# Selective-scan macaron block: the state sums of two scan units issued as a pair

## The chip, the core and the metric

The kernel runs on one core of a Trainium2 chip. The metric is the device time of one execution in microseconds (us), the median of three runs. The core's engines work from queues of their own, each in order: TensorE (PE, with its weight loads PEld), VectorE (DVE), ScalarE (ACT), GpSimd (POOL) and SyncE (SP), which issues nearly all the transfers. They wait for one another by semaphores.

## What is computed

The input x has 4 sequences of 1024 tokens with 512 channels, in fp32. Three stages follow one another, each added to its input:

```python
x = x + 0.5 * ffn(layernorm(x))        # gate/up 512 -> 1408, silu(g) * u, down 1408 -> 512
x = x + attn(layernorm(x))             # the selective scan below
x = x + 0.5 * ffn(layernorm(x))        # the same weights again
# attn, for I = 1024 inner channels and N = 16 states:
h, gate = split(x @ W_in.T); h = silu(conv4(h) + conv_b)
ts, Bm, Cm = rms-normed parts (128, 16, 16) of h @ Wx.T
delta = softplus(ts @ Wdt.T + dt_bias)
s[t] = exp(delta[t] * A) * s[t-1] + delta[t] * Bm[t] * h[t]     # for each channel and state
y[t] = sum over the 16 states of s[t] * Cm[t]  + D * h[t]
out  = (y * silu(gate)) @ Wout.T
```

The line that matters here is the sum over the 16 states.

## The kernel before

The 4096 tokens are cut into 16 blocks of T = 256 (NCS = 16, four to a sequence). The inner channels are cut into NI = 8 tiles of 128. The scan lays four states of 32 channels on the 128 partitions (Q = 32, S = 4), so a tile i of a block k needs NS = 4 groups g of states; one `unit(k, i, g)` handles 4 states of all 128 channels, as four strips of 32 channels. A block has 32 units, the kernel 512.

A unit (L553 to L587) goes, in two halves: ACT makes exp(delta * A) into the PSUM tile `da` (L569), POOL makes delta * B * u into `sb` (L572), DVE scans along the tokens in place in `da` (`tensor_tensor_scan`, L576), ACT keeps the last column as `state` (L581), and DVE multiplies by C into the unit's tile `pr` (L584). `pr` has four buffers, `da` four halves. The unit is then put on the list `summed`.

`add_up` (L591 to L600) takes the oldest unit off that list. PE sums its states: four matmuls, one per strip j, of the 128 x 32 matrix `fold` against 256 columns of `pr`; each writes 32 partitions of the PSUM tile `yps`, in which the four g of a tile accumulate (L594). The two halves of `yps` alternate from tile to tile. Behind the fourth g, DVE adds D * u and brings the result to `u` (L600). `gated` (L604, POOL) multiplies by the silu of the gate.

Beside the scan of block k stands a background (`background`, L694): the products of the first FFN for later token tiles and of the second FFN for earlier ones (gate L269 with its eviction by ACT at L283, up L269 with DVE at L300, down L315 with DVE at L323), the gate part of W_in for the block (gp, L541, eviction L545), the output product of block k-1 (op, L623, L627), and the preparation of block k+1: transposes of the normed input (L231), the conv part of W_in (hp, L372) with its first tap on ACT (L376) and three more on DVE (L383), the product with Wx (sp, L407), its norm (ACT L425, POOL L428 to L430, DVE L436), transposes (L449, L450) whose results DVE copies (L451, L452), and `head`, the softplus with the product dp (L486). Products take PSUM from three buffers (`ps_m`).

The loop at L792 to L823 sets the order: it issues a unit, then perhaps a sum, then as many pieces of the background as keep pace with the work done, by costs in PE and DVE work. A recording layer then schedules the instructions of each engine from that order, so that single matmuls may change places with their neighbours. Before, `BEHIND = 2` (L33): a sum is issued behind the unit that is two further on.

```python
                if len(summed) > BEHIND:
                    add_up()
```

The list is not emptied between blocks, only at the end of the last one (L824).

Of the kernel before, what the change touches and what calls it, by code (L numbers as in the profile page):

```python
# [29 lines left out]
BC = 2 * N  # L30
RO = R + BC
HEAD = 10
BEHIND = 2  # L33
LEAD = 12
BEGUN = 7
RING = 14
# [3 lines left out]
def macaron_kernel(ctx: ExitStack, tc: tile.TileContext, a: dict, out: bass.AP):  # L40
# [119 lines left out]
    def settle():  # L160
        while deferred:
            deferred.pop(0)[1]()

    def do(w):
        if w.settled:
            settle()
        before = list(deferred) if w.cost else []
        if w.blocks:
            got = given.pop(id(w))
            assert len(got) == len(w.blocks)  # L170
            w.emit(got)
        else:
            w.emit()
        passed(before)
        held.pop(id(w), None)
        fetch()
        for x in stores:
            x[0] += 1
        write(2)
# [293 lines left out]
    def head(k, i):  # L473

        d = st[k]
        nm = f"{k}_{i}"
        dp = ps_m.tile([P, 2, T], F32, tag="mm", name=f"dp{nm}")
        z = p1.tile([P, 2, T], F32, tag="z", name=f"z{nm}")
        e = p1.tile([P, 2, T], F32, tag="e", name=f"e{nm}")
        lg = p1.tile([P, 2, T], F32, tag="lg", name=f"lg{nm}")  # L480
        dd = p2.tile([P, 2, 2, T], F32, tag="dd", name=f"dd{nm}")
        de = dd[:, :, 0, :]

        def products():
            for q in range(2):
                nc.tensor.matmul(  # L486
                    dp[:, q, :], lhsT=w_dt[:, (i + q) * P : (i + q + 1) * P], rhs=d["tsT"],
                    start=True, stop=True,
                )

        def split():
            for q in range(2):
                b = dt_b[:, i + q : i + q + 1]
                pin(nc.scalar.activation(z[:, q, :], dp[:, q, :], AF.Abs, bias=b))
                pin(nc.scalar.activation(dd[:, q, 0, :], dp[:, q, :], AF.Relu, bias=b))

        def logs():
            pin(nc.scalar.activation(z, z, AF.Exp, scale=-1.0))  # L498
            pin(nc.scalar.activation(lg, z, AF.Ln, bias=1.0))

        def correct():
            pin(nc.gpsimd.tensor_tensor(e, e, z, ALU.subtract))
            pin(nc.gpsimd.tensor_tensor(lg, lg, e, ALU.subtract))

        def complete():
            pin(nc.gpsimd.tensor_tensor(de, de, lg, ALU.add))
            pin(nc.gpsimd.tensor_tensor(dd[:, :, 1, :], de, d["u"][:, i : i + 2, :], ALU.mult))
            d["dd", i] = dd[:, 0]
            d["dd", i + 1] = dd[:, 1]

        return [
            products,
            split,
            logs,
            lambda: None,
            lambda: None,
            lambda: pin(nc.gpsimd.tensor_scalar(e, z, 1.0, 1.0, ALU.add, ALU.subtract)),  # L517
            correct,
            complete,
        ]  # L520

    def rows(k, i):
        row = st[k]["row", i] = dram4.tile([S, Q, 2 * T], F32, tag="row", name=f"row{k}_{i}")
        load(out=row.rearrange("j p t -> (j p) t"), in_=st[k]["dd", i].rearrange("p a t -> p (a t)"))

    def spread(k, i):
        rep = st[k]["rep", i] = p2.tile([P, S, 2, T], F32, tag="rep", name=f"rep{k}_{i}")
        for s in range(S):
            load(
                out=rep[s * Q : (s + 1) * Q].rearrange("p j a t -> p j (a t)"),  # L530
                in_=st[k]["row", i].rearrange("j p t -> p j t"),
            )
# [20 lines left out]
    def unit(k, i, g):  # L553

        d = st[k]
        rep = d["rep", i]
        first, last = k % CPB == 0, k % CPB == CPB - 1
        nm = f"{k}_{i}_{g}"
        b0 = i * S
        if g == 0:  # L560
            d["yp"] = yps[:, i % 2, :]
        yp = d["yp"]
        pr = p4.tile([P, S, T], F32, tag="pr", name=f"pr{nm}")
        for h in range(0, S, 2):
            hs = slice(h, h + 2)
            da = ps_a.tile([P, 2, T], F32, tag="da", name=f"da{nm}_{h}")
            sb = p4.tile([P, 2, T], F32, tag="sb", name=f"sb{nm}_{h}")
            for j in range(2):
                nc.scalar.activation(  # L569
                    da[:, j, :], rep[:, h + j, 0, :], AF.Exp, scale=a_w[:, b0 + h + j, g : g + 1]  # L570
                )
            nc.gpsimd.tensor_tensor(  # L572
                sb, rep[:, hs, 1, :], d["bc"][:, g : g + 1, :].to_broadcast([P, 2, T]), ALU.mult
            )
            for j in range(2):
                nc.vector.tensor_tensor_scan(  # L576
                    da[:, j, :], da[:, j, :], sb[:, j, :],
                    0.0 if first else state[:, b0 + h + j, g : g + 1], ALU.mult, ALU.add,
                )
            if not last:  # L580
                nc.scalar.copy(state[:, b0 + h : b0 + h + 2, g : g + 1], da[:, :, T - 1 : T])  # L581
            if chores:
                chores.pop(0)()
            nc.vector.tensor_tensor(  # L584
                pr[:, hs, :], da, d["bc"][:, NS + g : NS + g + 1, :].to_broadcast([P, 2, T]), ALU.mult
            )
        summed.append((k, i, g, yp, pr))  # L587

    summed = []

    def add_up():  # L591
        k, i, g, yp, pr = summed.pop(0)
        for j in range(S):
            nc.tensor.matmul(  # L594
                yp[j * Q : (j + 1) * Q, :], lhsT=fold, rhs=pr[:, j, :],
                start=(g == 0), stop=(g == NS - 1),
            )
        if g == NS - 1:
            u = st[k]["u"][:, i, :]
            nc.vector.scalar_tensor_tensor(u, u, d_w[:, i : i + 1], yp, ALU.mult, ALU.add)  # L600

    def gated(k, i):
        u = st[k]["u"][:, i, :]
        pin(nc.gpsimd.tensor_tensor(u, u, g_all[:, i, :], ALU.mult))  # L604
        st[k]["gated", i] = True
# [167 lines left out]
    for k in range(NCS):  # L773
        more = k + 1 < NCS
        parts, n, done, vector = list(beside_scan[k]), 0, 0, 0
        total = sum(w.cost for w in parts) + units * unit_t
        total_v = sum(w.vector for w in parts) + units * unit_v
        upto = parts.index(ready[k]) + 1 if more else 0
        length = len(parts)
        if "spread" not in st[k]:  # L780
            settle()

        def step():
            w = parts.pop(0)
            do(w)
            return w.cost, w.vector

        def ahead(tiles):

            return k + (i + tiles) // NI, (i + tiles) % NI  # L790

        for i in range(NI):  # L792
            for g in range(NS):
                unit(k, i, g)
                if i == 0 and k:
                    gated(k - 1, NI - NS + g)
                if len(summed) > BEHIND:
                    add_up()
                n += 1
                done, vector = done + unit_t, vector + unit_v  # L800
                while parts and (
                    done * total_v < vector * total
                    or (length - len(parts)) * (units - HEAD) < upto * min(n, units - HEAD)
                ):
                    c, v = step()
                    done, vector = done + c, vector + v
                k2, i2 = ahead(2)
                if i % 2 == 0 and g == 2 and k2 < NCS:
                    assert not chores
                    rows(k2, i2)  # L810
                    rows(k2, i2 + 1)
                k2, i2 = ahead(3)
                if i % 2 == 1 and g == 1 and k2 < NCS:
                    while more and i2 == 0 and ready[k] in parts:
                        c, v = step()
                        done, vector = done + c, vector + v
                    chores += head(k2, i2)
                    chores.pop(0)()
            k2, i2 = ahead(2)
            if k2 < NCS:  # L820
                spread(k2, i2)
            if i >= 4:
                gated(k, i - 4)  # L823
        while summed and not more:  # L824
            add_up()
        if not more:
            for i in range(NI - NS, NI):
                gated(k, i)
        for w in parts:
            do(w)  # L830
# [63 lines left out]
```

## Time and profile before

| what | value |
|---|---|
| median of 3 runs | 3323.13 us (3322.13 to 3327.34) |
| the profiled execution | 3324.85 us, of which the span of its instructions is 3323.0 us |
| mean granted TensorE clock | 0.975 |
| front (first FFN tiles, no scan) | 0 to 173 us |
| block 0 / block 1 | 203 us / 175 us (first sum to the next block's first sum) |
| blocks 2 to 13 | 189 to 205 us each |
| block 14 / block 15 | 171 us / 161 us |
| end (second FFN of the last tiles) | 129 us: PE 121.6 busy |
| sums (L594), all | 4096 records, 370.4 us busy on PE |
| scans (L576) | 2048, 1371.4 us busy on DVE |

A fp32 matmul leaves two records on PE, so a sum of four matmuls is "x8" in the trace; transposes leave one. Busy times of PE are those of the records, whose ends are modelled; the start of a matmul is measured. A line of a block's busy times gives the stretch in us, its length, then busy time and number of records for PE, PEld, DVE, ACT and POOL, the granted clock, the share of the DMA engines and GB/s. In a line of waits stand the waiting instruction, the awaited one, the total in us, how often, and the longest.

### The profile page before, as it was taken

The page shows a single profiled execution, that of the slowest core. Times are in us where ns is not written, and L with a number is a line of the kernel's source. Part 1 is how long each engine was busy: PE and PEld are TensorE (multiplying, and loading weights), DVE is VectorE, ACT ScalarE, POOL GpSimd, SP SyncE. Part 2 cuts the span into 40 slices and gives each one's busy share as a digit, 9 for nine tenths or more (in the row PEclk, how much of TensorE's full clock was granted, in tenths as well). Part 3 has the DMA queues.
Part 4 walks back from the last instruction along what each step waited for, and adds up shares of the span by engine and source line. Part 5 has one row for each costly group of instructions (what it writes and reads, how often), then busy time and mean ns, then how long its engine had stood idle before and what let it go on. Part 6 is the DMA issues. An engine that isn't in the chain of part 4 may idle for free.

```text
span 3323.0 us, 41725 instructions
## 1 busy us (share of the span) xinstructions
PE 3129.9 (94%) x12448; PEld 1615.6 (49%) x12448; DVE 2441.5 (73%) x4213; ACT 1877.0 (56%) x4300; POOL 1952.8 (59%) x1895
## 2 busy tenths in 40 slices
PE   8897688999999999999999999999999999988799
PEld 6534353545445444544545454454545454554434
DVE  2176697887778778787968778786877878698831
ACT  3445565746576564756556475665647465666430
POOL 1255667566666657567665756666575666667520
PEclk9988798999999999999999999999999999999899
DMA  7335466556466565545656555656555564556521
GB/s 238 109 92 136 124 175 169 159 135 180 124 171 168 169 168 144 161 132 172 162 161 174 146 156 131 185 149 172 161 159 157 133 187 128 173 166 171 165 92 45
DMA packets 287425, 506.42 MB, mean 152 GB/s; under 512 B 32096, under 2 KB 50272, under 8 KB 287200
## 3 DMA queue, kind: packets, MB, share of 16 engines
q1 hardware_dynamic: 285616, 503.31, 54.2%
q8 instruction: 100, 1.64, 0.2%
q14 instruction: 125, 1.02, 0.1%
q10 hardware_dynamic: 1584, 0.45, 0.1%
HBM read 442.03 MB, written 61.60 MB: 152 GB/s over the span
## 4 chain that ended last, share of the span: by engine, by line
PE 68%; DVE 18%; ACT 7%; POOL 3%; issue 3%; DMA 1%; SPq 0%; ACTq 0%; DVEq 0%; POOLq 0%
PE fo L315 15%; PE gate_w L269 13%; DVE da L576 10%; PE up_w L269 8%; PE gp L541 6%; PE yps L594 6%; PE op L623 6%; PE hp L372 5%; DVE pr L584 4%; ACT da L569 2%; PE dp L486 1%; DVE hd L300 1%; PE gate_we L269 1%; POOL sb L572 1%; PE foe L315 1%
## 5 line engine op out<-in xcount | busy, mean ns | idle before, releaser
L572 POOL TENSOR_TENSOR sb<-rep,bc 128x512 f32<-128x512 f32 x1024 | 1284.7, 1274 | 804.3 <-DVE da L576 639.8
L576 DVE TENSOR_TENSOR_SCAN da<-da,state,sb 128x256 f32<-128x256 f32 x1536 | 1049.7, 737 | 199.9 <-ACT da L569 161.1
L569 ACT ACTIVATE da<-rep,a_w 128x256 f32<-128x256 f32 x2048 | 902.2, 473 | 268.7 <-DVE pr L584 253.5
L584 DVE TENSOR_TENSOR pr<-da,bc 128x512 f32<-128x512 f32 x1024 | 660.2, 676 | 90.6 <-ACT state L581 81.1
L269 PE MATMUL gate_w<-fxT,w_gate_w 128*128 128x512 f32 (+1 forms) x1408 | 592.4, 566 | 8.4 <-ACT g L545 3.5
L269 PE MATMUL up_w<-fxT,w_up_w 128*128 128x512 f32 (+1 forms) x1408 | 577.4, 561 | 4.4 <-PE hp L372 3.4
L315 PE MATMUL fo<-w_down_w,hd 128*128 128x512 f32 x1276 | 563.5, 597 | 0.0
L594 PE MATMUL yps<-pr,fold 128*32 128x256 f32 x4096 | 370.4, 399 | 109.1 <-DVE pr L584 102.6
L269 PEld LDWEIGHTS gate_w<-fxT,w_gate_w 128*128 128x128 f32 x1408 | 266.6, 194 | 272.6 <-issue 233.9
L581 ACT COPY state<-da 128x2 f32<-128x2 f32 x768 | 120.2, 164 | 492.0 <-DVE da L576 483.3
L269 PEld LDWEIGHTS up_w<-fxT,w_up_w 128*128 128x128 f32 x1408 | 263.3, 192 | 271.5 <-issue 231.8
L315 PEld LDWEIGHTS fo<-w_down_w,hd 128*128 128x128 f32 x1276 | 239.8, 192 | 283.9 <-issue 278.8
L576 DVE TENSOR_TENSOR_SCAN da<-da,sb 128x256 f32<-128x256 f32 x512 | 321.7, 679 | 61.3 <-ACT da L569 48.1
L594 PEld LDWEIGHTS yps<-pr,fold 128*32 128x32 f32 x4096 | 108.6, 110 | 403.0 <-DVE pr L584 176.7
L372 PE MATMUL hp<-mxT,w_W_in 128*128 128x259 f32 x1024 | 241.2, 388 | 6.7 <-issue 2.5
L541 PE MATMUL gp<-mxT,w_W_in 128*128 128x256 f32 x1024 | 246.0, 388 | 0.8 <-ACT g L545 0.5
L623 PE MATMUL op<-w_Wout,u 128*128 128x512 f32 x512 | 230.7, 600 | 6.3 <-POOL sb L572 2.6
L517 POOL TENSOR_SCALAR e<-z 128x512 f32<-128x512 f32 x64 | 124.4, 1943 | 175.9 <-ACT z L498 167.6
L383 DVE SCALAR_TENSOR_TENSOR u<-hp,conv_w,u 128x256 f32<-128x256 f32 x384 | 176.2, 474 | 66.0 <-ACT u L376 61.0
L372 PEld LDWEIGHTS hp<-mxT,w_W_in 128*128 128x128 f32 x1024 | 190.8, 190 | 59.8 <-issue 21.0
L541 PEld LDWEIGHTS gp<-mxT,w_W_in 128*128 128x128 f32 x1024 | 188.3, 190 | 61.6 <-issue 22.9
L283 ACT ACTIVATE hd<-gate_w,gate_s 128x512 f32<-128x512 f32 (+1 forms) x176 | 113.9, 648 | 137.1 <-PE gate_w L269 136.9
(112 smaller groups left out, 2592.9 us busy)
## 6 DMA issues: line engine op xcount, KB each, us to landing
rep<-row SPq DMA_DIRECT2D x512, 256.0 KB, 5.4
w_W_in<-in_W_in_dram SPq DMA_DIRECT2D x256, 256.0 KB, 3.2
w_gate_w<-in_gate_w_dram SPq DMA_DIRECT2D x198, 256.0 KB, 4.0
w_up_w<-in_up_w_dram SPq DMA_DIRECT2D x198, 256.0 KB, 3.5
w_down_w<-down_w SPq DMA_DIRECT2D x187, 256.0 KB, 3.0
row<-dd SPq DMA_DIRECT2D x128, 256.0 KB, 3.0
w_Wout<-in_Wout_dram SPq DMA_DIRECT2D x128, 256.0 KB, 3.1
bc<-bcd SPq DMA_DIRECT2D x64, 256.0 KB, 5.3
```

Source lines behind the costliest of these rows:

```text
L269: nc.tensor.matmul(o[:, : self.n], lhsT=w[:, k, :], rhs=self.xT[:, k, : self.n], start=(k == 0), stop=(k == KH - 1),)
L315: nc.tensor.matmul(op, lhsT=self.hd[:, it, t * P : (t + 1) * P], rhs=wd[it], start=(it == 0), stop=(it == NF - 1),)
L372: nc.tensor.matmul(hp[:, : K - 1 + T], lhsT=w[:, kk, :], rhs=st[k]["xnT"][:, kk, :], start=(kk == 0), stop=(kk == KH - 1),)
L383: pin(nc.vector.scalar_tensor_tensor(u[:, i, :], hp[:, q : q + T], conv_w[:, i, q : q + 1], u[:, i, :], ALU.mult, ALU.add,))
L517: lambda: pin(nc.gpsimd.tensor_scalar(e, z, 1.0, 1.0, ALU.add, ALU.subtract)),
L541: nc.tensor.matmul(gp[:, :T], lhsT=w[:, kk, :], rhs=st[k]["xnT"][:, kk, K - 1 :], start=(kk == 0), stop=(kk == KH - 1),)
L569: nc.scalar.activation(da[:, j, :], rep[:, h + j, 0, :], AF.Exp, scale=a_w[:, b0 + h + j, g : g + 1])
L572: nc.gpsimd.tensor_tensor(sb, rep[:, hs, 1, :], d["bc"][:, g : g + 1, :].to_broadcast([P, 2, T]), ALU.mult)
L576: nc.vector.tensor_tensor_scan(da[:, j, :], da[:, j, :], sb[:, j, :], 0.0 if first else state[:, b0 + h + j, g : g + 1], ALU.mult, ALU.add,)
L584: nc.vector.tensor_tensor(pr[:, hs, :], da, d["bc"][:, NS + g : NS + g + 1, :].to_broadcast([P, 2, T]), ALU.mult)
L594: nc.tensor.matmul(yp[j * Q : (j + 1) * Q, :], lhsT=fold, rhs=pr[:, j, :], start=(g == 0), stop=(g == NS - 1),)
L623: nc.tensor.matmul(op, lhsT=st[k]["u"][:, i, j * P : (j + 1) * P], rhs=wo[i], start=(i == 0), stop=(i == NI - 1),)
```

## The change

`BEHIND` is 1, and two sums are issued in a row when three units are on the list. After units 0, 1, 2 the sums of 0 and 1 are issued, after unit 4 those of 2 and 3, and so on: the sum of an even unit stays behind the unit that is two further on, that of an odd unit comes behind the next one. As each tile has four units, the pairs are g = 0, 1 and g = 2, 3 of a tile.

```diff
-BEHIND = 2
+BEHIND = 1
...
-                if len(summed) > BEHIND:
+                if len(summed) > BEHIND + 1:
+                    add_up()
                     add_up()
```

`add_up` itself is unchanged, so the skip term (L600) moves with the fourth sum of its tile. The lines behind L797 are one further down in the changed kernel; the lines of the functions above keep their numbers.

## Prediction

> **What bounds the kernel now.** I read the page's busy times and slices first, then the busy times of single blocks, then the chain that ended last, then the waits. Times are us; "block k" runs from its first sum matmul (L594) to the next block's.
>
> ```profile
> PE 3129.9 (94%) x12448; PEld 1615.6 (49%) x12448; DVE 2441.5 (73%) x4213; ACT 1877.0 (56%) x4300; POOL 1952.8 (59%) x1895
> ...
> PE   8897688999999999999999999999999999988799
> ...
> PEclk9988798999999999999999999999999999999899
> ```
>
> TensorE (PE) is full from slice 8 to slice 33, at full clock; before and after that it has holes, and the clock drops where it has them. The busy times by block (length, PE, PEld, DVE, ACT, POOL; the clock after them) separate the two kinds:
>
> ```profile
> 376.00:551.00 175.00, 136.10 (x622) 76.20 (x622) 149.68 (x262) 106.71 (x273) 124.18 (x122) 0.87 0.57 159
> 1139.00:1331.00 192.00, 189.18 (x756) 94.92 (x756) 152.79 (x260) 117.19 (x282) 120.21 (x117) 1.00 0.57 158
> ...
> 2862.00:3033.00 171.00, 146.29 (x697) 88.48 (x696) 136.64 (x240) 104.89 (x261) 111.58 (x106) 0.93 0.60 169
> 3033.00:3194.00 161.00, 137.74 (x583) 71.04 (x584) 130.15 (x215) 80.19 (x163) 98.27 (x83) 0.93 0.51 152
> ```
>
> Block 5 (second line), like all of 2 to 13, lasts as long as its matmuls: 189.2 of 192. Blocks 1, 14 and 15 leave PE 23 to 39 idle; there the scan chain sets the pace. In the full blocks the chain that ended last shows what PE's time is made of (start, length, what):
>
> ```profile
> 1352.40 0.57 PE yps L594 x8
> 1352.97 3.63 PE gate_w L269 x8
> 1356.60 0.57 PE yps L594 x8
> ...
> 1386.78 3.43 PE gate_w L269 x8
> ...
> 1488.29 1.00 PE yps L594 x16
> ```
>
> Each fp32 matmul leaves two records, so x8 is one unit's sum (four matmuls of 32 columns). One sum costs 0.57, two in a row 1.00 (further down the chain three cost 1.43): 0.43 per sum and 0.14 per group. And eight gate records take 3.63 after a sum, 3.43 when none stands before. A group of sums thus costs more than its sums. By the starts of single instructions: the last wide matmul ahead of a group is 523 ns from the group's first one instead of 429 (+94), a group is 136 ns plus 433 per sum, and the first matmul behind stands 533 from its follower instead of 429 (+104). Together **0.334 per group**, whatever it holds.
>
> Here the Trainium skill speaks against both readings. "Trainium Kernel Development and Optimization", Performance Expectations, calls matmul busy time "a bad metric" since matmuls are pipelined, and wants the weight loads' share; that is 49% here, by which PE would have half its time free and the change would give about 0 (3324.9). The row decides: inside a product the starts are an even 429 apart, each weight load (0.19) is followed by 0.24 of waiting for that beat, and the chain stays on PE from 1459 to 1559 without one other engine. And for the price: "TensorEngine Tiling", Key Properties, says only that a change of tiling mode drains the array; the one figure near it, the semaphore tail in "TensorE: Matmul & The Clock Gate" (25 + 4.7 per tile + 26.3 per increment), makes an estimate of 70 ns for four tiles and one increment. 106 groups would be worth 7.4 by that, 35.4 by the row. I take the row; it was measured on this very pattern.
>
> **What the change removes.** No instruction is removed or added; SP's order of DMAs is identical, so no transfer moves in its queue. Odd units' sums (g = 1, 3) are issued one unit earlier, even ones where they were. Laid side by side, the two programs have 407 groups of sums on PE before (the trace counts 407 too) and 293 after. Blocks 2 to 13: 289 and 183, that is 106 fewer, 9 (in two blocks 8) each. Blocks 0, 1, 14, 15: 30, 28, 26, 34 against 26, 26, 23, 35.
>
> *Full blocks, ceiling:* 106 x 0.334 = 35.4.
>
> *Merges that buy nothing.* PE isn't alone at its limit. In block 5 (same columns):
>
> ```profile
> 1230.00:1263.00 33.00, 32.39 (x123) 15.40 (x121) 32.78 (x57) 17.19 (x52) 19.45 (x28) 1.00 0.56 138
> ...
> 1280.00:1299.00 19.00, 19.00 (x77) 8.42 (x76) 6.70 (x11) 4.51 (x10) 7.65 (x9) 1.00 0.22 77
> ```
>
> From 1230 on VectorE is at 99%, and PE then stands 0.69 and 0.70 idle at 1263.1 (transposes behind L436) and 1266.5 (dp behind L451). Between its wait for conv tile 4 at 1218 and that dp, VectorE's own work sets the time; what PE saves there turns into a longer wait. Two of a block's merges lie there, units (4,0)+(4,1) and (4,2)+(4,3): 24 x 0.334 = 8.0 lost, leaving 27.4. Behind dp PE sets the pace again: at 1280 VectorE has 35% to do and waits 7.1 for fo at 1295. The merges in units 0 to 2 and 7 lie in that part, up to the next block's conv.
>
> *Conv tiles.* In block 7 hp2 starts only 0.2 behind the last tap (L383) of hp0, whose PSUM buffer it takes, and VectorE is full from 1189 to 1209. The merge ahead of it brings 0.334, of which about 0.13 is waited away: 12 x 0.13 = 1.6 lost. If all of it is lost there with the next one, 12 x 0.67 = 8.
>
> *PSUM.* Products rotate through three buffers, and where a group goes, the next product comes up to 0.77 nearer to the eviction of the third before it. I take 0: that eviction ends 3.9 earlier in the median, over 1.3 in 85 of 100 cases, and the tight ones are the conv tiles above and those ahead of the transposes. Without this cover each merge would lose its 0.33, which is rival 2.
>
> *New waits of the moved sums.* A sum waits for its products (L584), and all of PE queues behind it. In blocks 2 to 13 the median sum starts 13 after its products; odd ones move ahead of 3.3 of matmuls on average, at most 10.3. Laying each move on that slack leaves under 0.2 missing anywhere, nearest at unit (4,1): 6.7 of slack, 6.9 of move. That cover is VectorE's lead; if it were gone, PE would wait in the stretch where it waits anyway. In all 12 blocks: 1.1 at most, inside that stretch, so 0. In blocks 0, 1, 14, 15 the slack is mostly nil; the same laying-out gives 11.2 of new waits, above all (15,0,1) and (15,0,3), 3.0 each, and 10.4 relieved: 0.8 lost, between -10 and +11.
>
> *Block 0.* From 191 to 268 its chain is PE's; three groups fewer there: 1.0 gained.
>
> *The other queue.* Behind the fourth sum stands the skip term (L600) on VectorE, which moves ahead by 2.7 of VectorE work on average, by 9.4 for tile 4, past the weighing (L436). While it waits, scans, taps and up-products queue behind.
>
> ```profile
> PEld yps L594 <- DVE pr L584: 176.7, 130, 13.0
> ...
> PE yps L594 <- DVE pr L584: 102.6, 57, 12.6
> ...
> DVE u L600 <- PE yps L594: 83.8, 52, 5.9
> ```
>
> (waiter, awaited: total, times, longest.) L600's wait averages 1.6. For tile 4 I take 0: VectorE finishes up_w 6 at 1255.05, PE has it done at 1251.75, so the sums directly behind it, 1.2 long, are over before L600 comes. L600 itself (0.39 to 0.48) then lies ahead of L436 and delays the transposes, but as much work leaves the way to L451, and dp comes no later. The other bound is a 1.6 wait, a rival below.
>
> *Sum:* 27.4 - 1.6 - 0.8 + 1.0 = 26.0. The profiled execution has a span of 3323.0 and 1.85 around it, 3324.85, 1.72 above the median of the runs. 3324.85 - 26.0 = 3298.9, on the median's scale 3297.1.
>
> **Rivals.**
> 1. *Every group counts:* the stretch with the full VectorE gets shorter too, for its up-products come earlier. 114 x 0.334 = 38.1: 3285. For it: PE's idle time there is only 1.4 per block. Against: VectorE has 0.2 left in 33.
> 2. *Nothing reaches the end:* the scan chain takes over once PE gives way. Only the merge in unit 7, in the stretch where VectorE waits for fo, would count: 12 x 0.334 = 4: 3319. For it: block 15 does its scan in 161 with less beside it, so the chain can't be far below 192. Against: the waits of VectorE for PE, up to 7.1, in each block.
> 3. *Slower: L600 waits in VectorE's queue.* Place: tiles 4 and 7 of each full block, moved by 9.4 and 7.5 of VectorE work while their sums move by 5 to 7. Price at the mean wait above: 2 x 1.6 x 12 = 38.4, less the 26.0: 12.4 slower, 3335.5. It decides from 26.0 / 24 = 1.1 per wait. Against: VectorE's lag behind PE, 3.3 at up_w 6.
>
> That the change does not do what it says is excluded by the order of PE: 114 groups are gone.
>
> **The numbers.** My forecast 0.62 (3289 to 3306 by the bounds above), rival 1 0.15, rival 2 0.13, rival 3 0.10. A measurement of this kernel can tell about 0.2% (6.6) from no change: faster means under 3316.5. Forecast and rival 1 are faster, with half of rival 2's weight (its own spread straddles the limit) less a little for bad cases of the forecast: 0.80; within 0.2% 0.11; slower 0.09. The range runs from rival 1 to the limit of rival 2's better half: 3284 to 3316.
>
> **What would show it.** L594: busy time on PE down, 293 groups, x16 at 1.00 as the usual piece of the chain. Full blocks near 189.8 instead of 192, blocks 14 and 15 unchanged within 3. PE's wait at the transposes of a full block longer, to about 1.4. "PE yps <- DVE pr" near 103. If blocks shrink by 3, rival 1; if "DVE u L600 <- PE yps" goes from 84 to over 120 and the blocks don't shrink, rival 3. I am wrong if PE shows new waits for evictions (L545, L283) where a sum used to fill the time.

## The result and the profile after

The changed kernel takes **3312.24 us** (median of 6 runs, 3308.76 to 3314.05) where the kernel before, run beside it, takes 3324.1 (6 runs, 3322.13 to 3327.34): a ratio of 0.9962, 95% interval 0.9950 to 0.9975. That is 12 us faster; 26 were forecast. The time lies inside the range that was given (3284 to 3316), but only because the range reached into rival 2, above the 3306 where the bounds of the forecast ended. The profiled execution has a span of 3309.3 (3323.0 before), 13.7 less, and takes 3311.11.

From the page of the changed kernel, its busy times, the PE slices, the granted clock and the shares of the chain:

```profile
PE 3101.8 (94%) x12448; PEld 1637.3 (49%) x12448; DVE 2435.7 (74%) x4213; ACT 1883.9 (57%) x4301; POOL 1950.3 (59%) x1895
...
PE   8897697999999999999999999999999999988799
...
PEclk9988898999999999999999999999999999999899
...
PE 54%; DVE 20%; ACT 9%; POOL 3%; issue 3%; DMA 1%; SPq 0%; DVEq 0%; ACTq 0%; POOLq 0%
```

and the last of these lines before:

```profile
PE 68%; DVE 18%; ACT 7%; POOL 3%; issue 3%; DMA 1%; SPq 0%; ACTq 0%; DVEq 0%; POOLq 0%
```

PE's busy time fell by 28.1, the span by half of that, and the slices say 9 from 8 to 35, as they did before (the prediction read 33). What changed is the chain that ended last: PE now has 54% of the span in it, before it had 68%. With the work saved on PE the chain has moved to the other engines. The waits of the changed kernel name the places (waiter, awaited: total, times, longest):

```profile
PEld yps L594 <- DVE pr L584: 177.4, 142, 10.5
...
PE yps L594 <- DVE pr L584: 102.5, 57, 10.1
...
DVE u L600 <- PE yps L594: 57.8, 43, 5.1
```

and the same view for PE alone:

```profile
PE t L449 <- DVE sn L436: 15.9, 14, 1.7
PE up_w L269 <- ACT z L494: 9.5, 12, 0.8
...
PE dp L486 <- DVE tsT L451: 7.3, 11, 1.9
```

of which the kernel before has

```profile
PE dp L486 <- DVE tsT L451: 10.9, 15, 1.3
...
PE t L449 <- DVE sn L436: 7.0, 11, 0.9
```

The sums' wait for their products is where it was (102.6), and the skip term waits less than before (83.8), so rival 3 is dead. In PE's list, the transposes wait longer than before and dp less; the line of the up products behind L494 (the eviction of dp), 12 times up to 0.8, one for each full block, is new.

Block 5, the block that the prediction cut up, runs now from 1132.70 to 1324.40 (first sum to first sum; columns as in the prediction):

```profile
1132.70:1324.40 191.70, 187.33 (x757) 96.59 (x756) 151.45 (x259) 117.92 (x281) 119.46 (x117) 1.00 0.57 158
...
1214.00:1258.00 44.00, 42.52 (x155) 21.70 (x153) 41.99 (x77) 26.30 (x72) 28.61 (x31) 1.00 0.54 144
```

(A number behind a product's name counts within its block, from 0: gate 10 is the last gate product, hp 2 the third conv product. A sum (2,3) is that of the unit with i = 2, g = 3.) PE has 1.9 less to do than before (189.18), but from first sum to first sum the block is only 0.7 shorter (192.4 before). The rest stands as idle time of PE. In the second line, the 44 ahead of the transposes, it idles for 1.5, and VectorE is busy for 95% of it. The chain shows more. First before, then after (start, length, what):

```profile
1209.27 3.43 PE gate_w L269 x8
1212.71 0.57 PE yps L594 x8
1213.28 3.71 PE hp L372 x16
1216.98 0.86 PE dp L486 x4
1217.84 1.86 PE yps L594 x32
...
1219.76 3.67 PE up_w L269 x8
...
1248.38 3.43 PE up_w L269 x8
...
1262.77 1.08 DVE sn L436 x6
```

```profile
1203.08 3.45 PE gate_w L269 x8
1206.55 0.69 ACT hd L283
1207.26 1.28 ACT L195
1208.56 1.49 ACT hd L195
1210.06 0.88 ACT L196
...
1211.36 1.02 ACT u L376 x2
1213.71 0.66 ACT z L498
...
1223.55 0.66 DVE da L576
...
1256.91 1.08 DVE sn L436 x6
1260.29 1.13 PE dp L486 x4
```

Before, the chain stayed on PE through gate, sum, conv product, dp, four sums and the up products till 1252.4. After, it leaves PE with the last gate product (gate 10, ends at 1206.5), goes over ScalarE (its eviction L283, a table load of 1.28 for the silu, the silu, a second load of 1.28, of which the chain counts 0.88, the conv taps, the softplus) to VectorE (scans, taps, products) and comes back to PE only at dp, 54 later. Yet from that eviction (L283) to the weighing (L436) it is 50.0 before (1212.74 to 1262.77) and 50.4 after (1206.55 to 1256.91): the second way was as long as PE's all the time. That is a reading of two chains; e11, e5 and e6 test it.

That divides each block in two, and I measured both parts in every trace by the starts of matmuls: **S**, from the last matmul of gate 10 to the first transpose (L449), and **R**, the rest, from there to the next gate 10. Twelve S and the eleven R between them lie in the full blocks. A sum that another product cuts in two counts twice in the table, since each part takes nearly the time of a whole one (in the trace before, a group of six records adds 0.760 to the time of the wide products around it, one of eight 0.767):

| kernel | ratio to before | S: groups, sums | S, us | R: groups, sums | R, us |
|---|---|---|---|---|---|
| before | 1 | 72, 108 | 607.9 | 199, 275 | 1551.6 |
| changed | 0.9962 | 36, 96 | 613.4 | 135, 286 | 1536.4 |
| e11, one pair | 1.0012 | 60, 96 | 607.9 | 199, 286 | 1555.8 |
| e12, two pairs | 1.0008 | 48, 108 | 613.7 | 199, 275 | 1548.0 |
| e2, pairs inside | 1.0023 | 36, 96 | 613.6 | 199, 286 | 1553.2 |
| e1, pairs outside | 0.9950 | 72, 108 | 607.8 | 135, 275 | 1535.2 |
| e4, one unpaired | 0.9950 | 48, 108 | 613.4 | 135, 275 | 1532.6 |
| e5, short last silu | 0.9982 | 36, 96 | 608.3 | 135, 286 | 1543.6 |
| e6, statistics later | 1.0253 | 36, 96 | 594.3 | 154, 294 | 1633.5 |
| e7, before, statistics later | 1.0368 | 72, 108 | 601.1 | 209, 278 | 1663.4 |
| e8, e1 with statistics later | 1.0262 | 72, 108 | 601.1 | 154, 283 | 1627.4 |
| e3, pairs later | 0.9998 | 60, 132 | 602.8 | 143, 261 | 1560.2 |
| e9, fours early | 0.9924 | 48, 108 | 613.4 | 121, 266 | 1530.9 |
| e10, fours outside | 0.9918 | 72, 108 | 608.7 | 121, 266 | 1532.8 |

In R the change works as computed: 64 groups fewer are 21.4, 11 more sums at 0.433 cost 4.8, which makes 16.6 less; it is 15.2 less. In S it took 36 groups and 12 sums away from PE, 17.2 in all, and S got 5.5 *longer*. The experiments ask why. S and R are read from one profiled execution of each kernel.

### The profile page after: what moved, and what is told of

Its sections match the earlier page's. It is cut to its first block, busy times and chain, and to the rows that moved or that the text cites. A ratio compares the mean times of both kernels' runs of the same rounds, so it can differ in the third digit from the quotient of the medians.

```text
span 3309.3 us, 41599 instructions
## 1 busy us (share of the span) xinstructions
PE 3101.8 (94%) x12448; PEld 1637.3 (49%) x12448; DVE 2435.7 (74%) x4213; ACT 1883.9 (57%) x4301; POOL 1950.3 (59%) x1895
## 4 chain that ended last, share of the span: by engine, by line
PE 54%; DVE 20%; ACT 9%; POOL 3%; issue 3%; DMA 1%; SPq 0%; DVEq 0%; ACTq 0%; POOLq 0%
PE fo L315 14%; PE gate_w L269 11%; DVE da L576 11%; PE op L623 6%; PE gp L541 5%; PE yps L594 5%; DVE pr L584 4%; PE up_w L269 4%; PE hp L372 3%; ACT da L569 2%; DVE hd L300 2%; POOL sb L572 1%; ACT L196 1%; PE gate_we L269 1%; ACT L195 1%
## 5 line engine op out<-in xcount | busy, mean ns | idle before, releaser
L584 DVE TENSOR_TENSOR pr<-da,bc 128x512 f32<-128x512 f32 x1024 | 664.0, 677 | 91.1 <-ACT state L581 85.0
L269 PE MATMUL gate_w<-fxT,w_gate_w 128*128 128x512 f32 (+1 forms) x1408 | 585.5, 562 | 10.9 <-ACT state L581 4.9
L594 PE MATMUL yps<-pr,fold 128*32 128x256 f32 x4096 | 352.5, 396 | 102.5 <-DVE pr L584 102.5
L594 PEld LDWEIGHTS yps<-pr,fold 128*32 128x32 f32 x4096 | 121.5, 110 | 342.8 <-DVE pr L584 177.4
L283 ACT ACTIVATE hd<-gate_w,gate_s 128x512 f32<-128x512 f32 (+1 forms) x176 | 113.9, 648 | 130.0 <-PE gate_w L269 129.5
```

Source lines behind the costliest of these rows:

```text
L269: nc.tensor.matmul(o[:, : self.n], lhsT=w[:, k, :], rhs=self.xT[:, k, : self.n], start=(k == 0), stop=(k == KH - 1),)
L584: nc.vector.tensor_tensor(pr[:, hs, :], da, d["bc"][:, NS + g : NS + g + 1, :].to_broadcast([P, 2, T]), ALU.mult)
L594: nc.tensor.matmul(yp[j * Q : (j + 1) * Q, :], lhsT=fold, rhs=pr[:, j, :], start=(g == 0), stop=(g == NS - 1),)
```

## The experiments

In the texts on record, "the changed kernel" is the one above; theory A is in each case the one held when the text was written. The intervals are 95% and stand for ratios to the kernel before; each kernel ran beside the kernel before on one chip (4 to 16 runs against 9 to 25).

**e1: the pairs only outside of the full stretch.**

```diff
-                    add_up()
+                    if not 3 * NS <= i * NS + g < 5 * NS + 2:
+                        add_up()
```

> Pairs only where PE sets the pace; from unit (3,0) to (5,1) of each block one sum at a time, so the merges (2,2)+(2,3), (4,0)+(4,1), (4,2)+(4,3) are undone. Theory A (a group is worth 0.334, but merges beside a busy ACT or DVE chain are paid back as waits of PE at up_w 0, at the transposes t and at unit (4,1)): full blocks have 219 groups against 289 before, 70 x 0.334 = 23.4 saved, about 5 of new waits at gate 7 and gp 4 stay, 2 gained outside: some 20 below the kernel before, 8 below the changed one. Theory B (every merge is worth the same, 12 us over 114 groups, 0.105 each, the rest of the price being an artefact of modelled ends): 78 groups fewer, 8 below the kernel before, 4 above the changed one.

Measured: 3306.63, ratio 0.9950 (0.9938 to 0.9963), 16.6 below before. It has 36 groups more than the changed kernel, 12.0 by their price, and is not slower: by the ratios 4 below it (A had 8), though the two intervals overlap. S is back at 607.8. A's 20 lies inside the interval, B's 8 does not.

**e2: the complement, pairs only inside.**

```diff
-                    add_up()
+                    if 3 * NS <= i * NS + g < 5 * NS + 2:
+                        add_up()
```

> The complement: pairs only from unit (3,0) to (5,1) of each block, that is (2,2)+(2,3), (4,0)+(4,1), (4,2)+(4,3). Theory A: full blocks 253 groups against 289, 12.0 saved, but the waits at up_w 0 (+9), t, dp and (4,1) (+10) come all the same: 5 to 9 above the kernel before. Theory B: 36 groups at 0.105: 4 below it.

Measured: 3331.21, ratio 1.0023 (1.0014 to 1.0033): 8.0 slower, as A said. Thirty-six groups fewer, and the kernel is slower than the one without pairs: S 5.7 longer, R 1.6.

**e11 and e12: e2 in its two parts.** To the kernel before, one pair per block was added, units (2,2) and (2,3); in e12 the two of tile 4 instead. `BEHIND` is 1 in both, and the second call of the pair stands under a condition:

```diff
-                if len(summed) > BEHIND:
+                if len(summed) > BEHIND + 1:
                     add_up()
+                    if 3 * NS <= i * NS + g < 3 * NS + 2:
+                        add_up()
```

(e12: `4 * NS + 2 <= i * NS + g < 5 * NS + 2`.)

> The kernel before with one pair per block only, units (2,2) and (2,3): in the full blocks 12 groups fewer, worth 4.0 by the price of a group. Theory A (the stretch from the last gate product to the transposes is set by ScalarE and VectorE, and PE's work in it is free; the pair carries one sum of 0.433 out of it, ahead of the last gate product, where PE sets the pace): that stretch keeps its length, the rest grows by 12 x 0.433 = 5.2, the kernel is 3 to 6 slower than before, and PE waits at the first up product for 9 to 10. Rival B (a merge is worth its price where PE is full in the profile): 4 faster.

> The kernel before with two pairs per block only, (4,0) with (4,1) and (4,2) with (4,3): 24 groups fewer, worth 8.0. Theory A (same stretch; the skip term L600 of tile 4, 0.39 to 0.48, now lies ahead of the weighing L436): the stretch grows by 0.3 to 0.5 a block, 4 to 6 in all, the wait at dp behind it gets shorter by about 4; 0 to 3 slower. Rival B: 8 faster.

Measured: e11 3327.66, ratio 1.0012 (1.0004 to 1.0020), by which it is 4.0 slower; e12 3326.85, ratio 1.0008 (0.9999 to 1.0016). Both are where A put them, and B's 4 and 8 faster lie outside both intervals. In e11 S keeps its 607.9 and R grows by 4.2: the sum (2,3), which stood behind gate 10, now stands ahead of it. (In the profiled execution the part ahead of the first S is 3.1 shorter, which A does not speak of; its span is 0.8 longer.) The timeline of e11 at this place (start, length, engine, what; in brackets the idle time before it and who ended it):

```profile
1210.76 0.69 ACT L283 ACTIVATE hd<-gate_w,gate_s 128x512 f32<-128x512 f32 x1 [2.87 <-PE gate_w L269]
1217.78 3.67 PE L269 MATMUL up_w<-fxT,w_up_w 128*128 128x512 f32 x8 [0.82 <-ACT z L494]
```

and of the kernel before:

```profile
1212.74 0.69 ACT L283 ACTIVATE hd<-gate_w,gate_s 128x512 f32<-128x512 f32 x1 [2.87 <-PE gate_w L269]
...
1219.76 3.67 PE L269 MATMUL up_w<-fxT,w_up_w 128*128 128x512 f32 x8
```

From the gate's eviction to the first up product it is 7.02 in both. What PE no longer does in between (0.57 of sum, and what surrounds it) it waits: 0.82. Behind gate 10 the sum cost nothing; ahead of it, where no other engine is in the way, it costs its time. From e11's waits:

```profile
PE up_w L269 <- ACT z L494: 9.7, 12, 0.8
```

In e12 the other thing is seen. Its timeline around the transposes, then that of before:

```profile
1254.60 0.47 DVE L600 SCALAR_TENSOR_TENSOR u<-u,d_w,yps 128x256 f32<-128x256 f32 x1
1262.02 1.16 DVE L436 SCALAR_TENSOR_TENSOR sn<-sp,rr,ln_w 128x128 f32<-128x128 f32 x6
1262.41 0.33 PE L449 MATMUL t<-ident,sn 128*128 128x128 f32 x1 [1.17 <-DVE sn L436]
...
1265.48 1.13 PE L486 MATMUL dp<-tsT,w_dt 128*128 128x256 f32 x4 [0.55 <-DVE tsT L451]
```

```profile
1262.69 1.16 DVE L436 SCALAR_TENSOR_TENSOR sn<-sp,rr,ln_w 128x128 f32<-128x128 f32 x6
1263.08 0.33 PE L449 MATMUL t<-ident,sn 128*128 128x128 f32 x1 [0.69 <-DVE sn L436]
...
1263.78 0.46 DVE L600 SCALAR_TENSOR_TENSOR u<-u,d_w,yps 128x256 f32<-128x256 f32 x1
...
1266.48 1.13 PE L486 MATMUL dp<-tsT,w_dt 128*128 128x256 f32 x4 [0.70 <-DVE tsT L451]
```

The skip term now lies ahead of the weighing, as the prediction said, and the transposes come later by its length: S is 5.8 longer, 0.48 per block. The same work is missing behind it: R is 3.6 shorter, and dp waits less. Together 2.2 longer with 24 groups fewer.

**e4: the changed kernel with only (2,2) and (2,3) taken apart.** The condition of e1, but `not 3 * NS <= i * NS + g < 3 * NS + 2`.

> The changed kernel with one of its pairs undone, (2,2)+(2,3), so that sum (2,3) stands behind gate 10 again. Theory A: 12 groups more cost 4.0, the wait at up_w 0 behind ACT's silu (10.3 in full blocks) goes back to 1.5: 4 to 5 below the changed kernel. Theory B: 12 groups more cost 1.3: 1 above it.

Measured: 3306.01, ratio 0.9950 (0.9937 to 0.9962), 17.2 below before and by the ratios 4 below the changed kernel. The two intervals overlap, so the times alone do not settle it; the runs themselves lie apart (3304.94 to 3308.17 here, from 3308.76 up there), and the trace agrees. The group of the up product on the page of the changed kernel, and then on that of e4 (busy, mean ns, idle before it, who ended most of it):

```profile
L269 PE MATMUL up_w<-fxT,w_up_w 128*128 128x512 f32 (+1 forms) x1408 | 574.8, 560 | 13.4 <-ACT z L494 9.5
```

```profile
L269 PE MATMUL up_w<-fxT,w_up_w 128*128 128x512 f32 (+1 forms) x1408 | 575.5, 561 | 4.4 <-PE hp L372 3.4
```

The wait is gone, S has not moved (613.4), and R is 3.8 shorter: of the 4.8 for the sums that came back behind gate 10.

**e5: the start of S.** If ScalarE sets the start of S, a shorter silu there must shorten S. The silu of the gates went in parts of 4, 4 and 3 tiles; here it goes in 4, 5 and 2.

```diff
-                    if it % 4 == 3 or it == NF - 1:
+                    if it in (3, 8, NF - 1):
```

> The changed kernel, with the silu of the gate tiles cut at 3, 8, 10 in place of 3, 7, 10: the last one, between gate 10 and the first taps of conv tiles 4 and 5 on ACT, covers two tiles in place of three (1.05 in place of 1.48, from the 1.91 and 1.48 of four and three tiles). PE's order in the full blocks stays as it is. Theory A (up_w 0 waits for ACT's chain from gate 10: eviction, table load, silu, table load, taps, dp): 0.43 less in each full block, wait at up_w 0 from 10.3 to about 5, total 5 below the changed kernel. Theory D (up_w 0 waits for DVE's taps or for the sums of tile 3 themselves): wait unchanged, total unchanged.

Measured: 3318.74, ratio 0.9982 (0.9975 to 0.9989), 6 slower than the changed kernel, where A had it 5 faster. The half that A speaks of is in the numbers. S is 5.1 shorter, 0.43 per block, near a third of the 1.49 that the silu of three tiles takes, and the wait at the first up product falls from 10.3 to 5.5. But R is 7.2 longer: the silu of five tiles, 2.34 with a table load of 1.28 ahead of it and another behind it, now lies ahead of the conv taps, and the conv product hp 2 waits 8.2 where it waited nothing.

**e6, e7, e8: the end of S.** VectorE has the statistics of the next norm to do (`bn_stats`, L205, and `bn_aggr`, L206) inside S. Held at their place in the written order, they come later. e6 does so with the changed kernel, e7 with the kernel before, e8 with e1.

```diff
-        nc.vector.bn_stats(stt, src)
-        nc.vector.bn_aggr(mv, stt)
+        pin(nc.vector.bn_stats(stt, src))
+        pin(nc.vector.bn_aggr(mv, stt))
```

> The changed kernel with the layernorm statistics (L205, L206) kept in program order on DVE, so that four bn_stats (0.59 each) no longer stand in the stretch where DVE is full, ahead of the transposes t and of dp. The scheduler then splits more sums: 203 groups in full blocks against 183, 10.1 dearer by the count of groups. Theory A (DVE's own work sets t, dp and the end of sum (4,1)): waits at t, at dp behind sum (5,0) and at (4,0) go from 33 to under 8; total 15 below the changed kernel. Theory E (t waits for the norm's chain over ACT and POOL, L425 to L430, whatever DVE does): those waits stay, total 10 above the changed kernel.

> The kernel before with the same statistics kept in program order: 300 groups in full blocks against 289, 4.1 dearer. Theory A: of its waits at t and dp (12.1 and 11.4) most go: some 15 below the kernel before. Theory E: 4 above it.

> Pairs only outside unit (3,0) to (5,1), and the statistics in program order: 239 groups in full blocks, 12.8 saved against the kernel before, where pairs outside alone saved 23.4. Theory A: waits at t and dp gone as well (23.5 in pairs outside): 10 to 13 below pairs outside. Theory E: 10 above it.

Measured: 3408.29, 3446.9 and 3412.04, ratios 1.0253 (1.0239 to 1.0267), 1.0368 (1.0354 to 1.0382) and 1.0262 (1.0248 to 1.0276). Neither theory has these times. They are lost elsewhere: the transposes of the next normed input come too early for the late statistics, as the waits of e6 show,

```profile
PE tpf L231 <- ACT xnf L214: 87.9, 17, 8.3
PE tpfp L231 <- ACT xnfp L214: 16.0, 2, 15.8
...
PE t L449 <- DVE sn L436: 1.4, 3, 0.8
```

(the first was 9.7 in the changed kernel, the second 9.2), so the totals say nothing of the question. S does. With that work off VectorE it is 6.8 shorter in the kernel before, 6.7 in e1 and 19.1 in the changed kernel, and the wait at the transposes, the third line, is 1.4 instead of 15.9: VectorE set its end. And now the merges inside are worth something: S is 594.3 with them and 601.1 without, 6.8 *less*, where it was 5.5 more.

**e3: pairs, but later.** `BEHIND` stays 2 in the changed kernel, so that no sum is issued earlier than before and the even ones later.

```diff
-BEHIND = 1
+BEHIND = 2
```

> BEHIND 2 with pairs: odd units' sums stay where they were before, even units' come one unit later, so nothing is issued earlier. Full blocks 216 groups, 20.5 of PE time saved by the count of groups. Theory A: the pair (2,2)+(2,3) stands behind gate 10, so no wait at up_w 0; the merges in the stretch where DVE is full still buy nothing (8): some 12 below the kernel before. Theory C (what eats the gain is that sums come early and hold PE for their products): none of that here, all 20 gained. Either is spoilt if the four buffers of pr, all in use before a pair, stop DVE: then slower than the changed kernel, with DVE waiting for PE at L584.

Measured: 3323.08, ratio 0.9998 (0.9990 to 1.0006): no change to the kernel before, and neither theory's number. What came is the case that the text set apart, slower than the changed kernel with VectorE waiting for PE at L584. The line of e3, then that of the kernel before:

```profile
DVE pr L584 <- PE yps L594: 27.0, 24, 2.1
```

```profile
DVE pr L584 <- PE yps L594: 7.9, 5, 2.4
```

With the buffers of `pr` in the way, e3 does not decide between A and C. Against C stands that the sums' wait for their products is the same in the kernel before and the changed one. R pays 24.8 less for its sums and is 8.6 longer. PE waits at dp 23.6 instead of 11.4, at hp 2 7.8, at the up product 9 6.5 and at hp 3 4.5 more. How much of these comes from the buffers I did not follow further.

**e9 and e10: fewer groups where PE sets the pace.** All four sums of tiles 0 and 1 go in one group, behind the first unit of the next tile (`pr` in a pool with five buffers instead of four; those lines are not shown), the pair of (2,2) and (2,3) is taken apart, and in e10 also those of tiles 3 and 4.

```diff
-                if len(summed) > BEHIND + 1:
-                    add_up()
+                at = i * NS + g
+                if g == 0 and i - 1 in (0, 1):
+                    while len(summed) > 1:
+                        add_up()
+                elif i not in (0, 1) and len(summed) > 2:
                     add_up()
+                    if not 3 * NS <= at < 5 * NS + 2:
+                        add_up()
```

(e10; e9 has `not 3 * NS <= at < 3 * NS + 2`.)

> All four sums of tiles 0 and 1 go in one group, behind the tile's last unit; the other tiles as in the changed kernel with the pair of units (2,2) and (2,3) taken apart. Full blocks: 180 groups instead of 195 of that kernel, and the price the sums pay goes from 241.8 to 232.5. Theory A (a group that goes in the stretch of tiles 0 and 1 is paid back in full as long as no eviction by ScalarE is in the way of the next product): 9 below the kernel with one pair taken apart, near 3297. Rival B (what is gained there is waited for at the next product whose buffer ScalarE has not yet cleared, gate 7 and gp 4, and PE waits for the last product of the four): no gain, 3306 or above, and the waits of PE at gate 7, gp 4 or behind the fold sums grow by the 9.

> As the last one, but the sums from unit (3,0) to unit (5,1), in the stretch where VectorE is full, single again. Full blocks: 204 groups, price 240.5. Theory A (a merge in that stretch is worth nothing either way): the same as the kernel with quads and pairs, within 3, and the waits at the transposes and at dp shorter by what the sums pay more. Rival B (merges there do reach the end): 8 slower than it.

Measured: e9 3299.43, ratio 0.9924 (0.9912 to 0.9937); e10 **3298.55**, ratio 0.9918 (0.9905 to 0.9932), the fastest of all, 27 below before and 15 below the changed kernel by the ratios. Taking the inner pairs apart again costs nothing, as A said: with 24 groups more, e10's S is 4.7 shorter and its R 1.9 longer than e9's. A's size for e9 (9 below e4) fits the times, but by luck as far as the traces go: R is 1.7 shorter than e4's, where 14 groups and 9 sums fewer would be 8.6, and S is the same. Of the 4.3 by which the span of e9 lies below that of e4, 2.6 lie outside S and R; of the 5.7 of e10 below e1, 4.2. There PE's wait for the products (PE yps <- DVE pr, the whole span) went from 103.0 in e4 to 72.9 in e9. No run has the fifth buffer alone, so whether that or the groups brought this is not shown. Rival B named gate 7 and gp 4 as the places of new waits; gate 7's shrank (7.5 to 0.9). Others came: hp 2 behind the sum (2,2) 6.8, op behind the sum (2,0) 12.6 instead of 6.5. By the ratios e9 and e4 lie 8.6 apart; what that has over the 4.3 of the profiled executions stays open.

## Why the prediction was wrong, step by step

**The price of a group** was right. 293 groups were counted, 183 in the full blocks; at 0.334 and 0.433 a sum they pay 237.8 there instead of 273.2, 35.4 less. Taken off the distances between the starts of matmuls in the trace after, that price leaves 0.0 to 0.3 in twelve blocks at every place where PE has nothing to wait for. The estimate of 7.4 for all groups, which the prediction had worked out from the semaphore tail in the Trainium skill ("TensorE: Matmul & The Clock Gate", The cost: per-tile semaphore tail) and set aside, is too small: R alone fell by 15.2, with 11 sums more in it.

**The step that failed is "PSUM. I take 0".** PE's waits in the full blocks, read from the starts of matmuls less that price, grew from 43.9 to 67.5, by 23.6, and of the 35.4 only 11.8 were left. By place: the stretch with the full VectorE 10.2 (the forecast had 8.0), the first up product behind the gates 8.8 (forecast 0), gate 7 and gp 4 behind ScalarE's evictions 4.9 (forecast 0). In the last two PE waits for an eviction; they make 13.7 of the 14.0 by which the full blocks missed the forecast of 25.8. The prediction had looked at the evictions' lead, found 15 of 100 within 1.3, and put all of these down to the conv tiles and the transposes. But the first up product of each block was one of them: it waited 0.13 in each full block even before, so its lead was nothing, and the 0.77 that the moved sum had filled became 0.83 of waiting. That this is the cost, e11 and e4 show. For gate 7 and gp 4 there is the trace alone, here gate 7 of block 5, which starts 0.05 behind the end of an eviction (it had waited 0.32 before):

```profile
1167.30 0.69 ACT L283 ACTIVATE hd<-gate_w,gate_s 128x512 f32<-128x512 f32 x1
...
1168.04 1.12 PE L269 MATMUL gate_w<-fxT,w_gate_w 128*128 128x512 f32 x2 [0.61 <-ACT state L581]
```

**"Block 5, like all of 2 to 13, lasts as long as its matmuls"** was the reading behind it. It is true of R and not of S. The chain before showed one way, PE's, through S; a second, over ScalarE's eviction, table loads, silu and taps and then VectorE, was as long. The prediction let the VectorE stretch begin at 1230, where VectorE's busy share reaches 99%; by the chain after, and by e5, it begins at gate 10's eviction, 17 earlier, on ScalarE, which is busy only 57% of the span.

**Merges that buy nothing:** 8.0 for 24 groups. Measured by S, 36 groups lie there, 12.0. And twelve sums left S, where they cost nothing, for R, where 11 of them cost 4.8 (e11: R 4.2 longer). With the 5.5 by which S grew and 1.4 of other things in R that makes 23.7 of the 33.4 that 100 groups fewer in S and R should have given; 9.8 was left (S + R: 2159.5 and 2149.7).

**The skip term of tile 4, 0,** was nearly right: it did delay the transposes (by 0.48 in e12) and dp came earlier by most of that, for a net 2.2 in e12's twelve blocks.

**Conv tiles, 1.6 lost:** not seen; hp 2 and hp 3 wait no longer than before. **New waits of moved sums, 0 in full blocks:** right as a sum, 102.5 against 102.6 over the whole span. **Outside the full blocks** the sum had 1.0 gained and 0.8 lost; the part ahead of the first S is 4.1 shorter, that behind the last S 0.2 longer. This gain was not forecast; without it the miss would be larger.

**The rivals.** Rival 2 had the mechanism, the chain goes over to the scan once PE gives way, but for whole blocks; it holds in about a quarter of each. The change ended between it and the forecast. The sign that the prediction named, new PE waits for evictions where a sum used to fill the time, is what came, though behind L494 in the main, and behind L283 and L545 for the smaller part. Of the other signs, the 293 groups are there and the wait at the transposes is near the 1.4 named for each block; the full blocks went from 192.6 to 191.7 on average, not to 189.8.

## What to carry to other kernels

Where the chain shows one engine without a break, I would measure the second-longest way through the same stretch, from one fork to the next join (here from a gate's eviction to the transposes, 50 us): work taken off the first engine counts only down to that, and an engine that is busy for 57% of the span can own such a way when its table loads and evictions stand in one row. Put small work where its engine waits anyway, and merge it where the engine does not; a merge that draws a sum out of the first kind of place into the second costs more (0.433) than it saves (0.334).

## What was not expected of the hardware

The price of putting four 32-column fp32 matmuls among 128-column ones held: 0.334 per group, measured on single sums before and found again on pairs and fours. The switch to the silu's table and back costs ScalarE 1.28 each time, at each of a block's silus (86 pairs of loads in the trace after); at gate 10 these two loads are 2.56 of the 7.0 from the eviction to the first up product.
